# Where two halves of a weight's preparation are issued: a GNN and FFN layer on one core

## The chip, the core and the metric

The kernel runs on one core of a Trainium2 chip. The metric is device time in microseconds (us), the median of several executions. A core has five engines that run their own instruction streams and wait for each other by semaphores: TensorE (PE; its weight loads are shown apart as PEld), VectorE (DVE), ScalarE (ACT), GpSimd (POOL) and SyncE (SP), which here only issues transfers. One further execution was recorded by the hardware profiler; all readings of the profile are from that one.

## The reference

384 nodes have 1,024 features each. An attention layer over a graph comes first, and a quantised feed-forward network (FFN) second, each with a layer norm ahead of it and a residual addition behind it.

```python
q = x @ wq.T + bq ; k = x @ wk.T + bk ; v = x @ wv.T + bv
q2 = q @ wiq.T + biq ; k2 = k @ wik.T + bik ; v2 = v @ wiv.T + biv   # 16 heads of 64
scores = q2 . k2 * 0.125 + mask            # mask: edge weights, -inf where there is no edge
out = softmax(scores) . v2 ; x = x + out @ wo.T + bo

xq = fake_quant(layernorm(x))              # int8 steps, one scale for the whole matrix
h = fake_quant(silu(xq @ Q(w_gate).T) * (xq @ Q(w_up).T))
x = x + h @ Q(w_down).T                    # Q: one scale per row = max|row| / 127
```

The FFN's weights are small (352 x 1,024 for gate and up, 1,024 x 352 for down). They too are quantised on the chip: per row the largest absolute value, a division, rounding to int8.

## The kernel before

**Stages.** The first 160 us compute the mask and the projections q, k, v and q2. Then come eight **pairs** of heads, p = 0 to 7, in one Python loop over p (line 716). Behind the pairs stand the output projection, the residual and the FFN. The change concerns the pairs, from about 169 to 303 us.

**One pair.** `scores` (line 641) yields twice: first it issues the score matmuls (L653) of the first two thirds of the rows, into four PSUM banks, and their mask additions with a row minimum on VectorE (L659) and exponentials on ScalarE (L663); at the second call it issues those of the last third, the reciprocals of the row sums (L671) and six scalings of e (L673). `weigh` (line 676) belongs to the pair before: it turns e (L683), copies it (L685), multiplies it by v2 (L691) and copies the result out (L695). Its steps are taken one at a time. Between them TensorE gets a **fill**: for even p `inner_v` (line 611), three accumulations of eight matmuls each (L627), each ended by an addition on VectorE (L633); for odd p `inner_k`, which is `project2` (line 193): k2 of the next two pairs in seven products of four matmuls (L204). The products' results alternate between two PSUM banks of the pool `ps_mm`, and the additions that read them (L215, L221, L232, L236, and L218 and L228 on ScalarE) free these banks. For `project2`, `left_sums` (L184, L186, L188) first makes sums of the two weight tiles on VectorE. `fill_to(m)` issues the fill up to m sixteenths. The last pair's fill is the start of the output projection (L701).

**Preparing the FFN's weights.** `ffn_weights` (line 544) is a generator over 14 blocks of weight rows, called u0 to u13 here: u0 to u2 gate, u3 to u5 up (1,024 columns; u2 and u5 have 96 rows, the others 128), u6 to u13 down (352 columns). It keeps the rows of two blocks loaded ahead, in three buffers, so that the load of a block (L554, on SP's queue) waits until the block three earlier has been read. `quantise_rows` is, on VectorE, a reduction (L529), a multiplication (L530) and a reciprocal (L532), then the int8 result w8b on ScalarE (L535), then a cast to bf16, wqi, on VectorE (L541; for u0 to u2 on ScalarE, L539). Then TensorE **turns** the block (L572, or L582 for down) and ScalarE copies it out (L573, L583, L584). The last four blocks, u10 to u13, are turned only after the pairs.

**One take.** `prepare(at)` takes one step of the generator: it turns the block quantised before, loads a row block, and quantises the next one. The places, in sixteenths of the fill, are 2, 6 and 12 in pair 0, 2 in pairs 1 and 3, 2 and 14 in the others; place 2 is ahead of the pair's own scores, place 14 ahead of its last third. The block `with tc.issue_after(ins)` keeps the VectorE instructions issued inside it behind `ins` in VectorE's queue. Here `ins` is `taken[-1]`, the newest mask addition L659.

**Who sets the order.** TensorE, SyncE and GpSimd keep the order in which the program issues (line 77). In the pairs VectorE and ScalarE are ordered by a planner, which goes by its own reckoning of what is ready, and among what is ready by the order of the program. [...]

## Time and profile before

| what | value |
|---|---|
| median of 3 executions | 367.88 us (367.84 to 368.76) |
| profiled execution, its own time | 368.65 us |
| its span, first to last instruction | 366.9 us |
| granted TensorE clock, mean | 0.997 |
| ScalarE, GpSimd busy | 118.6 us, 74.1 us |

The busy time in four stretches of the pairs, in us:

| stretch | length | TensorE | VectorE | ScalarE |
|---|---|---|---|---|
| 183.0 to 198.0 (most of pair 1) | 15.0 | 14.39 | 10.15 | 8.59 |
| 198.0 to 217.5 (pair 2) | 19.5 | 19.50 | 13.55 | 10.80 |
| 217.5 to 233.0 (pair 3) | 15.5 | 15.50 | 8.97 | 7.85 |
| 233.0 to 251.0 (pair 4) | 18.0 | 18.00 | 11.14 | 8.77 |

Rows of a timeline are: start in us from the span's start, length, engine, line, operation, what it writes and reads, shape, how many in a row, and in brackets the idle time ahead of it with what ended it. [...] the next one on the same engine may start before it ends. "wmx" is the result of the reduction, "wrs" the reciprocal, "wqi" the block ready to be turned, "tp" the bank that it is turned into.

### The profile page before, as it was taken

What the parts mean: (1) busy time and instruction counts of PE and PEld (TensorE: products, weight loads), DVE (VectorE), ACT (ScalarE), POOL (GpSimd) and SP (SyncE); (2) the same over time, 40 slices, a digit from 0 to 9 for tenths busy, and PEclk for the clock granted to TensorE, in tenths of its full rate; (3) what the DMA queues carried; (4) which work ended last, traced back from release to release, by engine and by line L of the source; (5) the groups of instructions that cost most, each with busy time, mean ns of one, the idle gap of its engine ahead of it and who ended that gap; (6) DMA issues with size and microseconds to landing.
All of it is one profiled execution on the core that took longest, in us unless ns stands there. A gap on an engine that the chain in (4) does not pass through costs nothing.

```text
span 366.9 us, 5811 instructions
## 1 busy us (share of the span) xinstructions
PE 357.4 (97%) x2092; PEld 297.8 (81%) x2092; DVE 251.8 (69%) x767; ACT 118.6 (32%) x274; POOL 74.1 (20%) x87
## 2 busy tenths in 40 slices
PE   8999999999999999999999999999999999999993
PEld 8999999999999999998877778686967445448761
DVE  5788888888889988967285755656594612088764
ACT  2352000000000002304472736454652532233741
POOL 5020354455444552340000000000000000000103
PEclk9999999999999999999999999999999999999998
DMA  7969433343333368711500520040595100000004
GB/s 235 404 191 404 164 116 115 118 136 116 115 115 117 115 184 260 233 22 46 157 20 2 177 94 20 2 155 13 200 396 182 53 0 0 2 0 0 3 1 172
DMA packets 17948, 44.50 MB, mean 121 GB/s; under 512 B 3278, under 2 KB 8672, under 8 KB 17536
## 3 DMA queue, kind: packets, MB, share of 16 engines
q1 hardware_dynamic: 14960, 39.06, 31.4%
q0 software_dynamic: 2672, 4.68, 4.3%
q10 hardware_dynamic: 288, 0.39, 0.3%
q8 instruction: 16, 0.26, 0.3%
q14 instruction: 12, 0.10, 0.1%
HBM read 41.91 MB, written 2.21 MB: 120 GB/s over the span
## 4 chain that ended last, share of the span: by engine, by line
PE 91%; DVE 3%; DMA 2%; ACT 1%; issue 1%; SPq 0%; POOL 0%; ACTq 0%; POOLq 0%; DVEq 0%
PE p L204 34%; PE mm L627 12%; PE mm L204 9%; PE sc L653 5%; PE sc L691 5%; PE tp L683 4%; PE sc L701 3%; PE mm L701 3%; PE mm L856 3%; PE mm L321 3%; DMA biv_b<-in_L_gnn_biv_dram 2%; PE tp L329 2%; PE sc L856 1%; PE mm L960 1%; PE x L960 1%; ACT x L944 1%
## 5 line engine op out<-in xcount | busy, mean ns | idle before, releaser
L452 POOL DMA_INDIRECT mask_d<-value,place x51 | 57.5, 1128 | 67.8 <-DVE place L449 47.5
L204 PE MATMUL p<-actT,wt 128*128 128x192 f32 x360 | 66.2, 327 | 0.2
L204 PEld LDWEIGHTS p<-actT,wt 128*128 128x128 f32 x360 | 59.5, 190 | 0.9 <-DVE actT L236 0.4
L627 PE MATMUL mm<-wt,actT 128*128 128x256 f32 x192 | 45.8, 384 | 0.0
L627 PEld LDWEIGHTS mm<-wt,actT 128*128 128x128 f32 x192 | 34.9, 190 | 7.8 <-issue 2.8
L663 ACT ACTIVATE e<-s,mn 128x384 f32<-128x384 f32 x48 | 29.0, 605 | 32.3 <-DVE mn L659 32.3
L826 POOL TENSOR_SCALAR minus<-row 128x1 f32<-128x1 f32 x3 | 0.7, 220 | 175.6 <-DVE row L823 175.6
L659 DVE CUSTOM_DVE_ANT_0 s<-sc,mask 128x384 f32<-128x384 f32 x48 | 24.6, 554 | 15.8 <-PE sc L653 15.8
L204 PE MATMUL p<-x_right,s 128*128 128x192 f32 x176 | 32.2, 326 | 0.0
L204 PE MATMUL p<-x_right,wt 128*128 128x192 f32 x176 | 32.2, 326 | 0.0
L204 PEld LDWEIGHTS p<-x_right,s 128*128 128x128 f32 x176 | 29.2, 190 | 0.0
L204 PEld LDWEIGHTS p<-x_right,wt 128*128 128x128 f32 x176 | 29.2, 190 | 0.0
L439 DVE SCALAR_TENSOR_TENSOR junk<-key_b,key,later 128x384 f32<-128x384 f32 (+3 forms) x51 | 27.6, 541 | 0.0
L685 ACT COPY eTs<-tp 128x384 f32<-128x384 f32 x48 | 20.5, 478 | 21.8 <-PE tp L683 21.7
L218 ACT COPY actT<-p 128x192 f32<-128x192 f32 x15 | 4.8, 319 | 63.7 <-PE p L204 63.7
L215 DVE SCALAR_TENSOR_TENSOR actT<-p,bias,actT 128x192 f32<-128x192 f32 x45 | 18.8, 417 | 8.3 <-PE p L204 6.0
L228 ACT ACTIVATE actT<-p,bias 128x192 f32<-128x192 f32 x15 | 6.3, 420 | 50.1 <-PE p L204 50.1
L683 PEld LDWEIGHTS tp<-ident,e 128*128 128x128 f32 x144 | 17.1, 141 | 4.5 <-issue 2.6
L653 PE MATMUL sc<-k,actT 64*128 64x384 f32 x96 | 20.1, 518 | 0.0
L683 PE MATMUL tp<-ident,e 128*128 128x128 f32 x144 | 19.7, 273 | 0.0
L204 PE MATMUL mm<-actT,wt 128*128 128x192 f32 x96 | 18.9, 330 | 0.0
L691 PE MATMUL sc<-eTs,actT 128*64 128x384 f32 x96 | 17.2, 495 | 0.0
(233 smaller groups left out, 589.6 us busy)
## 6 DMA issues: line engine op xcount, KB each, us to landing
wt<-in_wq_dram SPq DMA_DIRECT2D x8, 512.0 KB, 10.8
wt<-in_wk_dram SPq DMA_DIRECT2D x8, 512.0 KB, 4.6
wt<-in_wv_dram SPq DMA_DIRECT2D x8, 512.0 KB, 3.9
wt<-in_wiq_dram SPq DMA_DIRECT2D x8, 512.0 KB, 3.6
wt<-in_wik_dram SPq DMA_DIRECT2D x8, 512.0 KB, 4.8
wt<-in_wiv_dram SPq DMA_DIRECT2D x8, 512.0 KB, 4.8
wt<-in_wo_dram SPq DMA_DIRECT2D x8, 512.0 KB, 6.8
actT<-in_x_dram SPq DMA_DIRECT2D x6, 512.0 KB, 4.2
```

Of the source, the lines that this page charges most:

```text
L204: nc.tensor.matmul(z, left[:, k * P : (k + 1) * P], r[:, k, :], start=(k == 0), stop=(k == HK - 1))
L215: nc.vector.scalar_tensor_tensor(dst, z, b, with_, op0=ALU.add, op1=ALU.add)
L439: nc.vector.scalar_tensor_tensor(junk[:, :left], keys[:, (c - k0) * P : (c - k0) * P + left], key[:, c : c + 1], later[:, :left], op0=ALU. ...
L452: ins = nc.gpsimd.indirect_dma_start(out=mask_d, out_offset=bass.IndirectOffsetOnAxis(ap=place[:, c : c + 1], axis=0), in_=value[:, c : c ...
L627: nc.tensor.matmul(pm, vT[:, k, t * P : (t + 1) * P], wt[k // HK][:, k0 : k0 + 256], start=(k == 0), stop=(k == KC - 1),)
L653: nc.tensor.matmul(ps[t, h], q2[hs, t * P : (t + 1) * P], k2[hs, :], start=True, stop=True)
L659: taken.append(nc.vector.tensor_tensor_reduce(s, ps[t, h], mask[:, t, :], -SCALE, 3.0e38, op0=ALU.add, op1=ALU.min, accum_out=mn[h][:, t : ...
L663: nc.scalar.activation(e[h][:, t, :], s, AF.Exp, bias=mn[h][:, t : t + 1], scale=-1.0, accum_out=sm[h][:, t : t + 1],)
L683: nc.tensor.transpose(pt[:, t * P : (t + 1) * P], e[h][:, t, m * P : (m + 1) * P], ident)
L685: nc.scalar.copy(eT[h][m], pt)
L691: nc.tensor.matmul(pav[h * D : (h + 1) * D, :], v2[:, m, c0 : c0 + D], eT[h][m], start=(m == 0), stop=(m == NT - 1),)
L701: nc.tensor.matmul(pm, outT[:, k, t * P : (t + 1) * P], wo[k][:, gs], start=(k == 0), stop=(k == KC - 1))
```

## The change

The generator's step is cut in two: one take quantises a block (with the row load ahead of it), the next take turns it. `turn_prepared(at)` and `quantise_prepared(at)` take them. Turns are issued at 6 and 12 sixteenths in pair 0, and at the old places in the others. The quantisation that stood at place 2 is issued, from pair 1 on, at 6 sixteenths, behind `freed[-1]`: the newest of the additions L221 and L633. The quantisation that stood at place 14 is issued after the last third of the pair's scores and the scalings of e, behind the newest L659, and ahead of the last step of `weigh`. Pair 0 quantises at its old places. Blocks u10 to u13 have an empty second step.

```diff
+    freed = []
     def project2(...):
...
         z = yield from product(s2, t2)
-        nc.vector.tensor_add(b1, z, a1)
+        freed.append(nc.vector.tensor_add(b1, z, a1).ins)
...
     def ffn_weights():
...
                 nc.scalar.copy(wT[:, :, i0 : i0 + rows], pt[:, :, :rows])
+                yield
             elif j >= KC - LATE:
                 quantise_rows(wn, P, I, wd_scale[:, j : j + 1], wq=wd_late[:, j - KC + LATE, :])
+                yield
                 yield
...
                 nc.scalar.copy(wdT[:96, 2, j * P : (j + 1) * P], pt[:96, 2, :])
+                yield
...
-                    nc.vector.tensor_add(v2[:, t, cs], pm, biv_b[:, cs])
+                    freed.append(nc.vector.tensor_add(v2[:, t, cs], pm, biv_b[:, cs]).ins)
...
-            def prepare(at):
+            def turn_prepared(at):
+                if at in ((6, 12) if p == 0 else (2,) if p in (1, 3) else (2, 14)):
+                    take(prep, 1)
+
+            def quantise_prepared(at):
                 if at in ((2, 6, 12) if p == 0 else (2,) if p in (1, 3) else (2, 14)):
                     if p or at == 12:
-                        with tc.issue_after(taken[-1]):
+                        with tc.issue_after(freed[-1] if p and at == 2 else taken[-1]):
                             take(prep, 1)
                     else:
                         take(prep, 1)

             fill_to(3 if p % 2 else 2)
-            prepare(2)
+            turn_prepared(2)
+            if p == 0:
+                quantise_prepared(2)
             next(sc)
             for j, m in enumerate((6, 9, 12)):
                 fill_to(m)
-                prepare(m)
+                turn_prepared(m)
+                quantise_prepared(m)
+                if p and m == 6:
+                    quantise_prepared(2)
                 take(wg, 1)
...
             fill_to(14)
-            prepare(14)
+            turn_prepared(14)
             run(fill)
             e_before = next(sc)
+            quantise_prepared(14)
             take(wg, 1)
```

## The prediction

> **What bounds the kernel now.** I read the page first, for the shares:

> ```profile
> PE 357.4 (97%) x2092; PEld 297.8 (81%) x2092; DVE 251.8 (69%) x767; ACT 118.6 (32%) x274; POOL 74.1 (20%) x87
> ```

> TensorE is busy for 357.4 of 366.9 us, and its order is written by hand. So any edit is worth what it adds to or takes from TensorE's waits. Next I read whom TensorE waits for, over the whole span. One of its four entries lies in the stretch that the change touches:

> ```profile
> PE mm L204 <- DVE k L221: 0.6, 1, 0.6
> ```

> It is one wait, in pair 1. The chain between 182 and 192 us shows what leads to it (start, length, what):

> ```profile
> 183.63 0.47 DVE s L659
> ...
> 184.11 1.13 DVE wmx L529
> 185.24 0.14 DVE rs L671 x2
> ...
> 185.43 2.00 DVE e L673 x6
> 187.42 0.07 DVE wrs L532
> ...
> 188.91 0.60 DVE wqi L541
> ...
> 189.99 0.28 DVE k L221
> 190.27 0.04 issue
> 190.32 1.57 PE mm L204 x8
> ```

> The reader is to see block u3's quantisation inside VectorE's queue: the reduction of its row (L529), its reciprocal (L532), its cast (L541), all ahead of the addition L221 that frees the bank. He is to see also what else happens: between L529 and L532 stand all six scalings of the last pair's e, because the planner orders VectorE by program order among what is ready, and the scalings come first in the program. A quantisation is therefore slow from end to end: L529 starts at 184.02, ScalarE's w8b at 187.58, 3.56 us later, and the cast ends later still.

> Then I looked, in order of time, at the places where a quantised block is turned. This is TensorE at the start of pair 3:

> ```profile
> 216.41 2.16 PE L691 MATMUL sc<-eTs,actT 128*64 128x384 f32 x12
> 218.50 1.57 PE L204 MATMUL mm<-actT,wt 128*128 128x192 f32 x8
> 219.91 0.49 PE L204 MATMUL mm<-k_right,s 128*128 128x192 f32 x2
> 220.23 0.51 PE L572 MATMUL tp<-ident_b,wqi 96*128 96x96 bf16 x8
> ```

> The block turned at 220.23 is u5 (the only ones 96 rows high are u2 and u5). Before the change it is quantised in the middle of pair 2, on VectorE and ScalarE here:

> ```profile
> 205.37 1.21 DVE L529 TENSOR_REDUCE wmx<-row 96x1 f32<-96x1024 f32 x1
> ...
> 208.42 0.69 DVE L541 CAST wqi<-w8b 96x1024 bf16<-96x1024 int8 x1 [1.26 <-ACT w8b L535]
> ```

> It has been ready for 11 us when TensorE comes to it.

> **The change, part by part.** *Instructions:* none is added or removed; the new yields cost nothing at run time. *TensorE's order:* following the takes through, each turn is still issued where it was (u2 at the start of pair 1, u3 and u4 in pair 2, u5 at the start of 3, u6 and u7 in 4, u8 and u9 in 5). Cost 0. *SyncE's order:* every row load keeps its place, for nothing else is issued on SP between old place and new; only its wait can end later. POOL has nothing here.

> *Quantisation at 2 goes behind the freeing addition* (u3, u4, u6, u7, u9, u11, u13). In pair 1, L530 and L532 (0.04 and 0.07) and the cast (0.60) leave the chain before L221. Of the reduction's 1.13 only about 0.2 leaves, since L671 waits for ScalarE's exponentials until 185.1 anyway. That is 0.9 us, and the wait is 0.6: gain **0.6**. Behind L221, u3's reduction holds up L215 (to 191.0, needed at 191.7), and w8b (1.15) comes before or after ScalarE's L228 (0.42), which product 6 needs at 193.1: from 0 to 0.4 lost. I take 0.1, the near end, because L228 is ready as early as w8b. In pair 2, u5's w8b no longer holds up the copies of e: the six turns of e at 208.94 take 0.79 where those at 206.55 take 0.66, gain **0.1**.

> *Quantisation at 14 goes behind the pair's last scores* (u5, u8, u10, u12), from behind the first four. Here the cover goes. The blocks u5 and u8 are turned 2/16 or 3/16 into the next pair, some 4 us after the scores that the quantisation now follows. In pair 3 (times of the trace before), VectorE's queue at this point reads now:

> ```profile
> 217.00 0.55 DVE L659 CUSTOM_DVE_ANT_0 s<-sc,mask 128x384 f32<-128x384 f32 x1
> ...
> 217.48 0.52 DVE L529 TENSOR_REDUCE wmx<-row 128x1 f32<-128x352 f32 x1
> ...
> 220.62 0.16 DVE L532 RECIPROCAL wrs<-wd_scale 128x1 f32<-128x1 f32 x1
> 221.48 0.34 DVE L541 CAST wqi<-w8b 128x352 bf16<-128x352 int8 x1 [0.70 <-ACT w8b L535]
> ```

> That is u6, not needed for another 14 us. u5 takes this very slot, and is needed at 220.23. Its working: reduction from 217.48; w8b 3.56 later (pair 1's chain, which has the same 1,024 columns) at 221.04; cast 1.18 after w8b starts (207.24 to 208.42 for u5 itself) at 222.22; plus 0.69 and 0.05 to TensorE (190.26 to 190.31): 222.96. Wait **2.7**. Behind the turn on TensorE stand the next four scores, so nothing of pair 3 on VectorE can run meanwhile. Bounds: if L530 and L532 went straight behind the reduction, w8b would start at about 219.1 and the cast end at 220.9 (wait 0.7) or, with the scalings ahead of the cast, at 221.6 (1.4). If the reduction itself came behind the scalings, the wait would be 3.5. I take 2.7, by six boundaries of this trace where the reduction goes first and L532 last.

> In pair 5 u8 (352 columns) is turned at 254.00. As u9 lies there now, its cast would start at 255.26 and end at 255.60: wait 1.65. But L695 (0.45) now follows the quantisation in program order, and the reciprocal should take the slot that L695 fills now, between the two heads' scalings (252.96); then the cast comes right behind the scalings, ends at 254.4, and the wait is 0.4. I take 0.6 before the next term. u10 and u12 are turned only after the pairs: 0.

> *What the row loads do to SP's queue.* A row load waits for w8b of three blocks earlier, and the next projection's weights are issued behind it:

> ```profile
> SPq L554 <- ACT w8b L535: 98.7, 8, 24.8
> ```

> In pair 2, u4's w8b goes from 202.95 to behind L633: TensorE's first third ends at 206.1, L633 0.35, reduction 1.13, 0.46 to w8b (as u7 and u8 show between reduction and w8b where VectorE is free), 1.15 long: 209.2. The wik loads go out at 209.6 instead of 204.52 and land at 214.9 instead of 209.83. left_sums then takes 1.93 (209.83 to 211.76), to 216.85, with L633's 0.35 behind it: pair 2's last score reduction starts at 217.2 instead of 216.52, **0.7** onto u5's wait. If the sums come behind the scalings instead, L188 pushes the cast by as much. The same reckoning for u7 in pair 4 gives 242.9 for the issue, 250.3 for the end of the sums, **0.3** onto u8's wait. The wiv, bo and wo loads behind u10 and u12 have 3 us or more in hand: 0.

> [...] TensorE will stand still for about 3.4 us. The last windows of the trace show what stillness does here (TensorE's last matmul ends at 360.63; the granted clock is the third number from the end):

> ```profile
> 363.00:364.00 1.00, 0.00 (x0) 0.00 (x0) 0.00 (x0) 0.00 (x0) 0.00 (x0) 1.00 1.06 390
> 364.00:365.00 1.00, 0.00 (x0) 0.00 (x0) 0.00 (x0) 0.00 (x0) 0.00 (x0) 0.92 0.24 81
> ```

> The clock held for 4.2 us (0.92 of that window, then 0.50). By this row a wait of 3.4 costs only itself. [...]

> **Sum:** -0.6 + 0.1 - 0.1 (pairs 1, 2) + 2.7 + 0.7 (pair 3) + 0.6 + 0.3 (pair 5) = **+3.7 us**. TensorE works without a gap from there to 340 us, so nothing absorbs it. The span goes from 366.9 to 370.6; the profiled execution's 368.65 (1.75 around its span) to 372.35. That execution is 0.77 above the median of 367.88, so the median goes to about **371.6**.

> **Rivals.** *(a) The turns wait as worked out:* 370.3 to 372.8; chance 0.60. *(b) Not slower: the chain runs straight through.* Place: VectorE right behind pair 2's last reduction. If the planner puts L530 and L532 ahead of the six scalings and the cast among them, u5 costs 0.7, u8 nothing, less 0.6: about 368.0, up to 368.9 with the scalings ahead of the cast. It decides once w8b starts within 1.7 us of the reduction's start. For it: the scalings are single instructions of 0.33, so the planner has gaps. Against it: L532 is late at all six boundaries. Chance 0.17. *(c) Weights late as well:* the sums fall between reduction and scalings, or TensorE waits for s2 first and for the cast after, or the clock drops: 5 to 7 us, 373 to 375; for it, L184 already waits 0.71 and 1.73 for wik; against it, 5 us of room. Chance 0.19. *(d) The change does only what it says:* -0.6, 367.2, if u5 is ready after all; chance 0.04. As w8b alone needs 1.15 and nothing can start before 217.5, little speaks for it.

> **Numbers.** What a measurement of this kernel can tell from no change is 0.3%, 1.1 us: 366.8 to 369.0. (a) and (c) lie above it, and a little of (b); most of (b) and (d) inside; beneath it only luck. Slower 0.80, same 0.18, faster 0.02. The range, 368.0 to 373.8, takes in (a) and (b) and leaves out (d) and the upper part of (c), less than 2 in 10; (a) alone has 370.3 to 372.8.

> **What would show it.** Right: no wait for L221 in pair 1; a wait of TensorE's turn L572 for wqi (L541) of 2.5 to 4 us at pair 3, and of L582 of 0.3 to 1.7 at pair 5; u5's L532 behind the scalings; clock 1.00. Wrong: L532 right behind L529 there; a wait for k L215 in pair 1 above 0.4; wik not later than 205.

## The result, and the profile after

The changed kernel takes 374.65 us in the median, against 368.32 for the kernel before in the same session: a ratio of 1.0153, with a 95% interval of 1.013 to 1.0175. It is slower by about 5.6 us. The ratios here and below leave out executions that lie more than 1.5% above the fastest of their kernel (here one of four, 379.99 us, with which the medians are 6.3 us apart). The direction was forecast, but the size was not: 371.6 was predicted, with 368.0 to 373.8 as range. The profiled execution took 374.46 us with a span of 372.7, so the sums below are made against a difference of 5.8 us of span.

Line numbers behind L190 have moved: L204 is now L207, L221 is L224, L529, L532, L535 and L541 are L532, L535, L538 and L544, the turns L572 and L582 are L576 and L588, and L633, L653, L659, L673, L695 and L766 are L640, L660, L666, L680, L702 and L783. Some of the variants further down shift them by a few lines more.

The list of TensorE's waits, of the changed kernel (engine, waiting line, what it waited for, total, times, longest):

```profile
PE tp L576 <- DVE wqi L544: 3.8, 1, 3.8
...
PE tp L588 <- DVE wqi L544: 1.2, 1, 1.2
```

The wait for L224 (L221 before) is gone. In its place stand the two waits that the prediction named, for u5 and for u8. The chain through the first of them (start, length, what):

```profile
214.75 0.69 DVE s L186
215.44 0.34 DVE actT L640
215.78 0.60 DVE wt L188
216.37 0.47 DVE s L666
...
216.85 0.47 DVE s L666
...
217.33 1.12 DVE wmx L532
218.45 0.15 DVE rs L678 x2
218.60 0.04 DVE w_scale L533
218.64 2.00 DVE e L680 x6
220.64 0.08 DVE wrs L535
...
220.79 1.16 ACT w8b L538
...
221.97 0.70 DVE wqi L544
222.67 0.05 issue
222.72 0.51 PE tp L576 x8
```

The reciprocal stands behind all six scalings, as in pair 1 of the kernel before, and the sums L186 and L188 are pushed up against the last scores. The timeline of TensorE shows something of which the trace of before has no example (start, length, engine, line, operation, shape, how many; idle time ahead of it in brackets):

```profile
222.72 0.51 PE L576 MATMUL tp<-ident_b,wqi 96*128 96x96 bf16 x8 [3.77 <-DVE wqi L544]
223.16 2.79 PE L660 MATMUL sc<-k,actT 64*128 64x384 f32 x8
```

The eight score matmuls behind the turn take 2.79 us; in pair 1 of the same execution they take 1.56. The stretches around it tell why (stretch, length, busy time and count of TensorE, of its weight loads, of VectorE, ScalarE and GpSimd, then the granted clock, DMA share, GB/s):

```profile
216.60:219.90 3.30, 2.35 (x14) 1.60 (x10) 3.30 (x13) 1.62 (x5) 0.00 (x0) 1.00 0.00 0
220.00:223.30 3.30, 0.58 (x10) 0.51 (x12) 1.85 (x5) 1.18 (x2) 0.00 (x0) 1.00 0.11 23
223.40:226.70 3.30, 3.30 (x11) 1.64 (x10) 1.77 (x7) 2.07 (x6) 0.00 (x0) 0.50 0.90 289
226.80:230.00 3.20, 3.20 (x24) 3.18 (x23) 1.77 (x8) 2.42 (x7) 0.00 (x0) 1.00 0.13 46
```

The clock is 0.50 for the third of them. The trace's clock record has it from 223.35 to 226.76, which is 3.41 us.

**Where the 5.8 us went.** TensorE runs the same 2,092 matmuls in the same order in both kernels, so the start of each can be compared with the start of its counterpart. Ahead of the pairs the changed kernel is 0.34 us early, which comes between 141 and 144 us, where the trace of before has a row load that lands later; the change does not aim at this stretch. By the end of pair 2 it is 1.44 early: the first move gained 1.1. At u5's turn it is 2.49 late, which is 3.9 for the wait (the expectations below have it as 3.85). Twenty matmuls later it is 4.14 late, which is 1.65 for the half clock. At u8's turn it is 5.6 late, which is 1.4 for that wait. (The listed waits are 3.77 and 1.23. They are shorter because the rows of successive matmuls overlap, 0.33 long and 0.16 apart in the products L207, and a matmul behind a stop has nothing to overlap with.) A last 0.2 comes in pair 6.

**How much of it the late weights made.** In the changed kernel's timeline the last mask additions of pair 2 start at 216.29. That of the kernel before has them at 216.52, and TensorE is 1.44 early here, so they are 1.2 later against TensorE. The weights for k2 went out at 208.44 instead of 204.52. So 1.2 of u5's 3.9 come from the late weights, and 2.7 from the chain behind the scores. In pair 5 the same comparison of the reduction (256.00 against 251.25, with TensorE 4.2 late) gives 0.55 of u8's 1.4.

### The profile page after: what moved, and what is told of

It reads as the page before. It is cut to its first block, busy times and chain, and to the rows that moved or that the text cites. A ratio compares the mean times of both kernels' runs of the same rounds, so it can differ in the third digit from the quotient of the medians.

```text
span 372.7 us, 5811 instructions
## 1 busy us (share of the span) xinstructions
PE 358.2 (96%) x2092; PEld 297.9 (80%) x2092; DVE 253.7 (68%) x767; ACT 118.6 (32%) x274; POOL 75.2 (20%) x87
## 4 chain that ended last, share of the span: by engine, by line
PE 86%; DMA 5%; DVE 5%; ACT 2%; SPq 0%; issue 0%; ACTq 0%
PE p L207 37%; PE mm L207 9%; PE mm L634 8%; PE sc L660 5%; PE tp L690 3%; PE sc L698 3%; PE sc L708 3%; PE mm L708 3%; PE mm L874 3%; PE mm L324 3%; DMA wt<-in_wik_dram 3%; DMA wt<-in_wq_dram 2%; PE sc L874 1%; DVE e L680 1%; PE mm L978 1%; PE x L978 1%
## 5 line engine op out<-in xcount | busy, mean ns | idle before, releaser
L455 POOL DMA_INDIRECT mask_d<-value,place x51 | 58.7, 1150 | 66.0 <-DVE place L452 45.8
L207 PE MATMUL p<-actT,wt 128*128 128x192 f32 x360 | 66.1, 327 | 0.0
L207 PEld LDWEIGHTS p<-actT,wt 128*128 128x128 f32 x360 | 59.6, 190 | 0.2
L666 DVE CUSTOM_DVE_ANT_0 s<-sc,mask 128x384 f32<-128x384 f32 x48 | 24.5, 554 | 17.9 <-PE sc L660 17.9
L207 PE MATMUL p<-x_right,wt 128*128 128x192 f32 x176 | 32.2, 327 | 0.0
L207 PE MATMUL p<-x_right,s 128*128 128x192 f32 x176 | 32.2, 327 | 0.0
L207 PEld LDWEIGHTS p<-x_right,s 128*128 128x128 f32 x176 | 29.2, 190 | 0.0
L207 PEld LDWEIGHTS p<-x_right,wt 128*128 128x128 f32 x176 | 29.2, 190 | 0.0
L221 ACT COPY actT<-p 128x192 f32<-128x192 f32 x15 | 4.8, 318 | 63.3 <-PE p L207 63.3
L660 PE MATMUL sc<-k,actT 64*128 64x384 f32 x96 | 21.3, 547 | 0.0
L207 PE MATMUL mm<-actT,wt 128*128 128x192 f32 x96 | 19.1, 332 | 0.0
L184 DVE TENSOR_TENSOR s<-wt 128x512 f32<-128x512 f32 x19 | 13.4, 705 | 7.3 <-DMA wt<-in_wik_dram 7.0
```

What stands on the lines that cost most here:

```text
L207: nc.tensor.matmul(z, left[:, k * P : (k + 1) * P], r[:, k, :], start=(k == 0), stop=(k == HK - 1))
L455: ins = nc.gpsimd.indirect_dma_start(out=mask_d, out_offset=bass.IndirectOffsetOnAxis(ap=place[:, c : c + 1], axis=0), in_=value[:, c : c ...
L660: nc.tensor.matmul(ps[t, h], q2[hs, t * P : (t + 1) * P], k2[hs, :], start=True, stop=True)
L666: taken.append(nc.vector.tensor_tensor_reduce(s, ps[t, h], mask[:, t, :], -SCALE, 3.0e38, op0=ALU.add, op1=ALU.min, accum_out=mn[h][:, t : ...
```

## The experiments

Three readings were to be told apart. **Mine after the result:** the second move makes TensorE wait for u5 and u8, and the clock falls because of the first wait. **Rival one:** the clock fell by chance or for another reason, and the waits alone are the loss. **Rival two:** the loss comes from the first move, whose later quantisation holds back the row loads on SP and with them the weights.

### The changed kernel again

No edit.

> The changed kernel once more, beside the others on the same chip. Theory: TensorE's two waits for quantised blocks (u5 about 3.8 us, u8 about 1.3) and one window at half clock behind the first, less about 1 us gained in pairs 1 and 2: +5 to +6.5 us against before; [...] Rival (the clock fell by chance once): about half of the executions at +4.

Measured: 376.34 us in the median, 374.48 to 379.4 over six executions, ratio 1.0232 (1.0203 to 1.0261). The profiled one, 374.48, waits 3.6 for u5 and 1.0 for u8, and its clock is 0.50 from 222.53 to 225.95. So the half window is no single accident. Half of the executions at +4, as the rival had it, did not come: none lies below +6. The median, +7.9, is above the upper end of what I expected too. The mean clock of each execution explains the spread only in part. In the longest, 379.4, it is 0.984, which is some 12 us at half clock against 6.8 in the profiled one; but 376.30 and 376.69 have 0.994 and 0.993, less time at half clock than the profiled one, and are 2 us longer.

### Filling the wait

```diff
                 pt = ps_tp.tile([P, KC, P], BF16, name="tp")
+                if u == 5:
+                    for _ in range(56):
+                        nc.tensor.transpose(pt[:, 0, :], ident_b, ident_b)
```

> The changed kernel with 56 idle transposes of the identity (about 3.1 us) ahead of u5's turn, which fill most of TensorE's wait; the turn still starts when its block is cast. Theory: the wait ends at the same time, the clock stays at 1.00, and 1.65 us come back: +4.1 against before, about 372.5. Rival, that the clock falls for another reason or that transposes do not count as work for it: unchanged, +5.8.

Measured: 373.01 us in the median (three of four executions between 371.61 and 373.05; a fourth took 471.26 at a mean clock of 0.754, and one of the kernel before took 467.24), ratio 1.0126 (1.0108 to 1.0144). TensorE's timeline of this kernel:

```profile
218.23 3.29 PE L577 MATMUL tp<-ident_b 128*128 128x128 bf16 x56
221.71 0.51 PE L579 MATMUL tp<-ident_b,wqi 96*128 96x96 bf16 x8 [0.18 <-DVE wqi L544]
222.15 1.56 PE L663 MATMUL sc<-k,actT 64*128 64x384 f32 x8
```

The turn starts no earlier than its block allows, and yet the scores behind it are back to 1.56 us. The clock of this execution is 1.00 from 354 to 367 us and 0.998 in the mean, against 0.991 in the changed kernel run again, and the three executions have mean clocks of 0.997 to 0.998. Work that computes nothing made the kernel faster by 3.3 us in the medians, or 2.9 between this profiled execution and that of the changed kernel run again. Of that, 1.5 lies between the turn and the tenth matmul behind it; 0.6 was there before the turn, and 0.65 came in pair 6. Rival one falls.

### Filling both waits

```diff
+                if u == 5:
+                    for _ in range(56): ...      # as above
...
                 pt = ps_tp.tile([P, 3, P], BF16, name="tp")
+                if u == 8:
+                    for _ in range(18):
+                        nc.tensor.transpose(pt[:, 0, :], ident_b, ident_b)
```

> The changed kernel with idle transposes in both waits: 56 ahead of u5's turn and 18 (about 1.0 us) ahead of u8's. Theory: both waits end when they did, no window of TensorE is idle enough to halve its clock, so what is left is the waits alone, less the gain: +3.5 to +4 against before in every execution, and the executions lie within about 1 us of each other instead of 5. Rival, that the spread has another cause: executions up to 376 and more.

Measured: 372.36 us, ratio 1.0117 (1.0102 to 1.0133), and all four executions lie between 372.11 and 372.69. Their mean clocks are 0.996 to 0.998. The spread is 0.6 where the changed kernel, run again, had 4.9. So most of the spread went with the idle time in the two waits. That it is the half windows alone is not shown: the filling of one wait, at mean clocks of 0.997 to 0.998, left a spread of 1.4, and these are four executions. The waits less the gain cost 4.2 us, a little more than the 3.5 to 4 expected.

### The second move undone for one block

```diff
             turn_prepared(14)
+            if p == 2:
+                quantise_prepared(14)
             run(fill)
             e_before = next(sc)
-            quantise_prepared(14)
+            if p != 2:
+                quantise_prepared(14)
```

> The changed kernel with one thing undone: in pair 2 the second quantisation (u5) stands at 14 sixteenths again, ahead of the last scores. Theory: u5's wait and the half clock go (3.85 + 1.65), u8's wait of 1.2 to 1.4 stays: +0.3 against before, about 368.6. Rival, that late wik loads and the first move make up the loss: still +3 or more.

Measured: 369.64 us, ratio 1.0031 (1.0014 to 1.0047), so +1.1 by the ratio where +0.3 was expected. In the profiled execution 0.35 of that stands at 148 us already, behind a wait of 1.4 for the first weights, which the edit does not touch. One block's place is worth 6.7 us in these medians. The wait for u8 stays, alone:

```profile
PE tp L588 <- DVE wqi L544: 1.1, 1, 1.1
```

and the mean clock is 0.995, against 0.992 in the profiled execution of the changed kernel.

### The second move alone

```diff
-                        with tc.issue_after(freed[-1] if p and at == 2 else taken[-1]):
+                        with tc.issue_after(taken[-1]):
...
             turn_prepared(2)
-            if p == 0:
-                quantise_prepared(2)
+            quantise_prepared(2)
...
-                if p and m == 6:
-                    quantise_prepared(2)
```

> Only the second move: the quantisation from place 14 goes behind the last scores, that of place 2 stays ahead of the pair's scores. Theory: pair 1's wait for L221 (0.6) is back; the weights for pair 3 are in time, so u5's wait is 2.7 to 3.0 instead of 3.85; u8's 1 to 2. +4 against before if the clock holds through a wait of 2.8, +5.7 if it falls. Rival, that the loss comes from the first move: less than +2.

Measured: 376.14 us, ratio 1.0207 (1.0182 to 1.0233). Rival two falls as an explanation of the loss: the second move alone makes all of it. At +7.8 the loss is larger than either figure expected. The waits are 2.7 for u5, 1.9 for u8 and 0.6 for L224. The stretches of this execution:

```profile
217.90:221.20 3.30, 1.66 (x10) 1.36 (x9) 3.27 (x14) 1.16 (x2) 0.00 (x0) 1.00 0.00 0
221.30:224.60 3.30, 2.31 (x18) 1.43 (x19) 2.16 (x7) 1.90 (x4) 0.00 (x0) 1.00 0.60 164
255.40:258.70 3.30, 1.37 (x11) 1.00 (x11) 2.22 (x11) 1.46 (x4) 0.00 (x0) 1.00 0.00 0
258.80:262.10 3.30, 3.30 (x11) 1.78 (x8) 2.34 (x9) 2.02 (x7) 0.00 (x0) 0.50 0.83 253
```

In the traces of the changed kernel and of the kernel before, the changes of the clock lie whole multiples of 3.413 us apart (worked out below). With this trace cut into windows of that length from its own changes of the clock, the longer wait, 2.7, is parted into 1.67 and 1.06, and the clock behind the first part, from 221.30, is 1.00. The shorter one, 1.9, falls into one window, and the clock from 258.80 is 0.50. So in this execution the longer wait was not followed by half clock, and the shorter was. Where the windows lie differs from trace to trace: the clock record begins at 4.89 us in the changed kernel and at 4.08 in its second run. That executions of one kernel differ by this would fit the five executions here (mean clocks of 0.993 and 0.994 with 375.18 and 374.49 us, 0.989 and 0.990 with 376.14 to 376.98), but is not shown: only one of them has a trace.

### The quantisation ahead of the scalings

```diff
-                if t < NT - 1:
-                    yield e
+                yield e                  # in scores(): also behind the last exponentials
...
-            e_before = next(sc)
+            next(sc)
             quantise_prepared(14)
+            e_before = next(sc)
```

> The changed kernel with the second quantisation issued between the last scores and the scalings of e, so that in program order its reciprocal and cast come first. Theory: u5's w8b starts 2 us after the reduction instead of 3.55 and its cast stands before the last scaling, u5's wait is 1.3 to 1.5, u8's 0 to 0.1, no half clock: +0.3 against before, about 368.7. Rival, that the wait is made by the place behind the scores alone: u5's wait above 3.

Measured: 374.17 us, ratio 1.0152 (1.0115 to 1.019). The chain in pair 3:

```profile
216.84 1.13 DVE wmx L532
217.97 0.14 DVE rs L677 x2
218.11 0.04 DVE w_scale L533
218.15 0.35 DVE e L679
218.50 0.07 DVE wrs L535
218.57 1.31 DVE e L679 x4
219.88 0.66 DVE wqi L544
220.54 0.05 issue
220.58 0.51 PE tp L576 x8
```

The reciprocal now stands behind one scaling instead of six, so the program's order does set VectorE's, and u8's wait is gone. But u5's wait is 2.1 and not 1.3 to 1.5, pair 6's scores wait 0.9 for the copy (L701 here), and the window behind u5's wait still runs at half clock (0.50 from 221.5 to 224.8). My expectation of +0.3 missed. In the traces the order of the scalings is worth about 1.7 of u5's wait and all of u8's. In the time little of it is seen: the ratio is that of the changed kernel's first measurement, 1.0153, and below that of its second, 1.0232.

### The weights ahead of the row load

```diff
-                wa, wb = (load_w("wik", p + j) for j in range(2))
+                wa, wb = wik.pop()
...
             e_before = next(sc)
+            if p % 2 == 0 and p < NP - 2:
+                wik.append([load_w("wik", p + 2 + j) for j in range(2)])
             quantise_prepared(14)
```

> The changed kernel with the next projection's weights issued ahead of the row load that waits for u4's (u7's) int8 result. Theory: left_sums is done before the last scores, u5's wait falls from 3.85 to about 3.2 and u8's from 1.3 to 1.0; +4.8 against before, or +3.2 where the clock holds. Rival, that the late weights cost nothing: +5.8 to +8 as in the changed kernel.

Measured: 374.61 us, 371.19 to 378.62, ratio 1.0126 (1.0083 to 1.0168). The profiled execution is the longest of the six, so its waits need not be those of the others:

```profile
PE tp L576 <- DVE wqi L544: 2.6, 1, 2.6
PE sc L661 <- DVE actT L703: 1.4, 1, 1.4
```

u5's wait falls by 1.2 and u8's, to 0.7, by 0.5, further than expected, and by what the changed kernel's own trace gives for the late weights. But a new wait of 1.4 appears in pair 2, of its scores for L703 (the copy L695 of before), with a half window behind it (0.50 from 205.0 to 208.3). Behind u5's wait two windows run at half clock, from 225.42 to 232.25, and TensorE loses 3.0 us by them. The interval of the ratio lies below that of the changed kernel's second measurement but overlaps that of its first, so what the late weights cost in all is left open.

### The first move alone

```diff
             turn_prepared(14)
+            quantise_prepared(14)
             run(fill)
             e_before = next(sc)
-            quantise_prepared(14)
```

> Only the first move: the quantisation from place 2 goes behind the freeing addition, that of place 14 stays ahead of the last scores in all pairs. Theory: no wait of TensorE in the pairs, pair 1's 0.6 and about 0.3 of pair 2 gained: -0.6 to -1.0, about 367.4. Rival, that the late weights of the next projection (issued behind the later row load) cost time: 0 to +2.

Measured: 369.93 us, ratio 1.0037 (1.0022 to 1.0053). I had expected a gain of 0.6 to 1.0; it is a loss of 1.5. The profiled execution took 372.88, the longest of the eight. TensorE's waits, VectorE's timeline and two stretches of it show a wait that the changed kernel does not have, and a half window behind it:

```profile
PE sc L660 <- DVE actT L702: 2.6, 1, 2.6
```

```profile
270.31 0.69 DVE L783 TENSOR_TENSOR actT<-actT,wt 128x512 f32<-128x512 f32 x1 [3.63 <-DMA actT<-in_x_dram]
```

```profile
270.00:274.10 4.10, 1.52 (x7) 0.36 (x4) 3.79 (x12) 0.00 (x0) 0.00 (x0) 1.00 1.02 416
274.20:277.50 3.30, 3.30 (x8) 2.67 (x9) 3.30 (x11) 2.50 (x8) 0.00 (x0) 0.50 0.75 304
```

In pair 6 VectorE stands for 3.63 us on the addition of x and bo, and the copy L702 that frees a bank for the scores is queued behind it and starts at 272.65. The weights and bo of pair 6 go out at 258.9 to 260.8 instead of 255.7 to 257.2, behind a row load that waits for u9's int8 result, and x lands 6.95 us after its issue, at 270.2. How much of this the seven shorter executions have is not recorded. That the loss of the median hangs on the row loads too, as rival two says, is what the next version tests.

### The first move with the row loads at the turns

```diff
-            if len(ahead) < len(units):
+            if u == 0:
                 load_row()
...
                 yield
+                next_row(u)              # load_row() for u > 0 while blocks are left
                 pt = ps_tp.tile(...)
```

> The first move alone, with each row load issued at the turn of the block two before it instead of at its quantisation, so that SP's queue no longer stands still for int8 results. Theory: the weights, bo and x of pair 6 are in time again, the wait of pair 6's scores for the copy L702 (2.6 in the first move alone) and its half clock are gone: -0.6 to -1.0 against before, 367.4 to 367.8. Rival, that the wait of pair 6 has to do with VectorE's order and not with the transfers: +1 to +2 as in the first move alone.

Measured: 368.46 us, ratio 1.0004 (0.9986 to 1.0023): the loss is gone, so it did hang on SP's queue, and rival two is right for the first move alone. The expected gain did not come either. L224 is waited for no more and TensorE is 0.8 us further ahead after pair 1, but it loses as much again in pair 2. There left_sums of the next projection, whose weights now come early, stands on VectorE between the scores and the scalings, and the copy (L709 here) is waited for.

### The first move in pair 1 alone

```diff
-                        with tc.issue_after(freed[-1] if p and at == 2 else taken[-1]):
+                        with tc.issue_after(freed[-1] if p == 1 else taken[-1]):
...
-            if p == 0:
+            if p != 1:
                 quantise_prepared(2)
...
-                if p and m == 6:
+                if p == 1 and m == 6:
                     quantise_prepared(2)
...                                       # place 14 as before the change
```

> The kernel before with the first move made in pair 1 alone (u3), every other block quantised at its old place. Theory: the wait for L221 goes, u5 and u8 have their old lead, SP's queue waits hardly longer than before, nothing of TensorE stands still in the pairs and no window runs at half clock: -0.6 to -0.8 against before, about 367.7. Rival, that a freed half microsecond is lost again to whatever the planner rearranges: 0.

Measured: 367.58 us, ratio 0.9985 (0.9977 to 0.9993). So it is faster than the kernel before by 0.54 us (0.3 to 0.8 by the interval), a little less than expected, and the fastest of all kernels measured here. Its chain through pair 1 has TensorE alone:

```profile
186.00 1.82 PE mm L207 x10
187.82 0.66 PE tp L690 x6
188.48 1.95 PE mm L207 x12
190.43 0.66 PE tp L690 x6
```

The four products run without a gap where the kernel before stood for 0.61.

## Why the prediction was wrong

**Point by point.** *TensorE's order unchanged, turns at their old places:* right, matmul for matmul. *Signs of being right:* the wait for L221 is gone, the turns wait 3.8 and 1.2, and the reciprocal stands behind the scalings, all as named; the last of them, clock 1.00, did not come. *Gain in pairs 1 and 2:* 0.6 net predicted, 1.1 measured. *u5's wait:* 2.7 for the chain and 0.7 for the late weights were predicted, 3.9 measured. The chain is as worked out: 5.4 us from the reduction to the turn, 2.7 of them as a wait. The late weights cost 1.2. Their loads went out 0.3 us later than put (208.44 here is 209.9 in the times of before) and the sums could start 5.6 us after that instead of 5.3. *u8's wait:* 0.9 predicted, 1.4 measured. The reciprocal did take the slot between the two heads' scalings, but L702 did not leave it for that; both stood there, and its 0.46 was added. The late weights cost 0.55 here, not 0.3.

**The step that failed is the clock.** The prediction went by the last windows of the trace and put the clock at nothing: "By this row a wait of 3.4 costs only itself." What came is a window at half clock, 1.65 us, and that is the largest part of the 2.1 us that the sum lacked. The two waits were 0.5 each too small, and the larger gain and the 0.34 us ahead of the pairs hid most of that.

The row was misread. The clock changes of a trace lie whole multiples of the half clock's 3.413 us apart: in the changed kernel from 4.89 to 223.35 are 64 of them, from 226.76 to 370.12 are 42. In the trace of before the clock record begins with 1.00 at 6.44 and falls to 0.50 at 364.84, 105 of them later. Counted back from there, windows of this length begin at 361.43 and 358.01 (an estimate, for the clock did not change there). These are windows of before:

```profile
360.00:361.00 1.00, 0.64 (x3) 0.19 (x1) 0.97 (x2) 0.58 (x1) 0.69 (x1) 1.00 0.66 258
361.00:362.00 1.00, 0.00 (x0) 0.00 (x0) 0.57 (x2) 0.37 (x1) 0.00 (x0) 1.00 0.46 180
...
365.00:366.90 1.90, 0.00 (x0) 0.00 (x0) 0.00 (x0) 0.00 (x0) 0.00 (x0) 0.50 0.00 0
```

TensorE ended at 360.63, inside such a window with only 0.8 idle, and the clock fell at the end of the next one. By this reading the 4.2 us were the rest of one window and a whole one, 0.8 and 3.41; they depend on where the stop lay, and are no measure of how long a stop leaves the clock at 1.00. With the 1.65 us that the changed kernel's trace shows, the sum would have been +5.4 or 373.3, inside the range that was given. The median of all four executions came out above that. One reason on record is the execution of 379.99: its mean clock of 0.984 is some 12 us at half clock (an estimate from its span of 378.2), against 6.0 in the profiled one, so by this estimate more than one window was halved there ahead of the end (the end alone has 2.1 us in the trace of before and 2.6 in that of the changed kernel). The rest of the scatter is open.

**The rivals.** (a) has the mechanism of the waits right, and without the clock its range would have held (5.8 less 1.65 is 4.15, or 372.0). (c), at a chance of 0.19, named "or the clock drops" and put it at 373 to 375. That is what came; its other two places did not, for the sums ended ahead of the last scores' mask additions and TensorE did not wait for s2. (b) and (d) did not occur: L535 stood behind the scalings in pair 3, and u5 was not ready.

**A step that was wrong without being seen in the result.** "The wiv, bo and wo loads behind u10 and u12 have 3 us or more in hand: 0" failed in the first move alone, at pair 6. There wiv and bo went out 3 us later, so that bo was 3.4 us ahead of x instead of 7.5, and wo followed x at 265.1; the price in the profiled execution was a wait of 2.6 and a half window. In the changed kernel bo was as close to x, 3.6 us, but wo went out only at 278.6, and x landed in 4.3 us. So wo behind x seems to have had part in it; no run tells the two apart.

## What to carry to other kernels

When TensorE is the bound and a step off its path is moved, compare the new distance from that step's end to its consumer with the whole chain between, including everything that program order puts among its pieces; here a chain of 1.1 + 1.2 + 0.7 us of real work took 5.4. Look behind a stop of TensorE for its price: here six stops with 1.93 to 3.15 us inside one window of 3.413 were followed by half clock, which cost another 1.65 us in the changed kernel, and 3.0 in the one case where two windows ran at half. A line at the end of a trace, where nothing follows, was weak evidence on such a price. And where only one place has the wait, try that one alone. Here that gave 0.54 us, and the versions that moved the same step in all pairs gained nothing or lost.

## What the runs showed of the hardware

**TensorE's idle time and the clock behind it.** I cut the traces into windows of 3.413 us, counted from their changes of the clock, and took TensorE's idle time in a window and the clock of the window that follows. Each value of the second column is one stop in one profiled execution.

| kernel | TensorE idle in the window | next window |
|---|---|---|
| end of TensorE's work, the window it ends in: changed kernel, kernel before | 0.26, 0.79 | 1.00 |
| u8's wait: the changed kernel again, changed kernel | 1.00, 1.23 | 1.00 |
| weights ahead of the row load, pair 2 | 1.42 | 0.50 |
| second move alone, u5 | 1.67 | 1.00 |
| second move alone, u8 | 1.93 | 0.50 |
| weights ahead of the row load, u5 | 2.11 | 0.50 |
| quantisation ahead of the scalings, u5 | 2.14 | 0.50 |
| first move alone, pair 6 | 2.51 | 0.50 |
| changed kernel, u5 | 2.78 | 0.50 |
| changed kernel again, u5 | 3.15 | 0.50 |
| end of TensorE's work, the window behind: changed kernel, kernel before | 3.41, 3.41 | 0.50 |

**How long the clock stayed at 0.50.** In the changed kernel it stayed for 3.41 us: TensorE was busy for all of the stretch from 223.40 to 226.70, and from 226.80 the clock is 1.00. In the weights ahead of the row load, behind u5's wait, TensorE stood for the first 0.45 us of the halved window, and the clock stayed at 0.50 for two, from 225.42 to 232.25, which is 6.83 us.

**The clock under transposes.** The 56 bf16 transposes of the identity took 3.29 us of a wait of 3.8. In the changed kernel 0.50 follows this wait; with them in it the scores behind it take 1.56 us instead of 2.79, and the mean clock is 0.998. In the kernel's first microseconds TensorE runs nothing but f32 transposes, from 1.34 us on. In the trace of before these start 0.213 us apart up to 6.31 and 0.109 apart from 6.48, and the clock record begins, with 1.00, at 6.44. In the changed kernel the step from 0.213 to 0.109 lies between 4.81 and 4.96, and the record begins at 4.89.
